# A graph layer with two ways to gather: compares one group ahead, picks ahead of the sums

## The chip, the core and the metric

The kernel runs on one core of a Trainium2 chip. The metric is the device time of one execution in microseconds (us), lower is better. TensorE multiplies matrices into PSUM, VectorE and ScalarE work element by element, GpSimd issues indirect DMAs here, and SyncE issues the other loads and the stores.

## What is computed

One layer of a graph network on 6250 nodes with 64 features and 206250 edges that are sorted by their destination:

```python
h = jnp.maximum(_layernorm(x, axis=-1), 0.0)
msg = jax.nn.relu(h[src] + edge_attr)
agg = jax.ops.segment_sum(msg, dst, num_segments=x.shape[0])
out = x + (jax.nn.relu((h + agg) @ W1 + b1) @ W2 + b2)
```

All of it is float32. The costly part is `h[src]`: a row of 64 numbers for each of 206250 edges.

## The kernel before, in words

The edges come in groups of 1024: 128 partitions by G = 8 columns, so a column is 128 edges. There are NG = 201 groups and a tail of 4 columns. For each group the edge features `ea` (SyncE) and the gathered source rows `xg` are brought to SBUF, into pools of LOOK = 10 buffers each.

A column's rows are fetched in one of two ways. `gather` (line 146) has GpSimd issue one indirect DMA per column from `h_rows`, the normalized nodes in DRAM. From group RAW = 4 on, the last columns of a group are left to TensorE: two in an even group, one in an odd one (`pool_cols`), 296 columns in all. They are called tiles here. For a tile, TensorE first turns the source numbers so that they lie along the free dimension (`spread`, line 304: a transpose into `turned`, a PSUM tile of 8 columns that is used as a ring). Then VectorE compares them with the numbers of all nodes (line 311), in four pieces (CUTS), and writes a 0/1 matrix `hot` of 49 blocks of 128 nodes. Then TensorE multiplies the 49 blocks with `hp`, the normalized nodes as three bf16 parts that add up to float32 (line 315, the picks). ScalarE puts the edge features of the tile beside the three parts as a fourth (line 360), and VectorE adds up the four (line 369).

For the other columns VectorE adds `xg` to the edge features in PSUM (line 367). ScalarE's relu makes the messages `msg` (line 371). They are summed by destination on TensorE: `one_hot` (line 341) compares the slot of each edge within a window of W = 64 nodes with the numbers 1 to 64, and 8 float32 matmuls (line 377) add the messages of a group into a PSUM window `agg`. VectorE adds the window to `z` at a place that is read from the data (line 336). The places of eight groups at a time are loaded into VectorE's registers (line 287). When all edges of a block of 512 nodes have been summed, `hidden`, `result` and `store` compute its output: two small products on TensorE, an add on VectorE (line 402), and a store; there are 12 such blocks and a rest of 106 nodes.

Each engine runs its instructions in the order of the program, and the program's order is the one that the Python code writes them in. Before the change, one step of the loop over groups is: add the last group's window to `z` and finish node blocks; `window_sum` (add, reduce, relu, sums of this group); `take` (load and copy the next group's edge features); `pick_group` (for each tile of the next group: turn the tile that comes four later, compare, pick); `one_hot` of the next group. The numbers 1 to 64 for the one-hot lie in PSUM (`wslots`).

Eight groups into the loop, `find_left` (lines 262 to 280) looks for edges outside their windows, which are done by another path if there are any; a step later the output bias is added to `x_sb` (line 433).

Of the kernel before, what the change touches and what calls it, by code (L numbers as in the profile page):

```python
# [9 lines left out]
F32 = mybir.dt.float32  # L10
I32 = mybir.dt.int32
I16 = mybir.dt.int16
BF16 = mybir.dt.bfloat16
# [6 lines left out]
P = 128  # L20
# [18 lines left out]
LAG = 1  # L39
AB = 4  # L40
KB = NB * R + 1
BIAS = 4096
# [8 lines left out]
def kernel(  # L51
# [62 lines left out]
    nc.vector.memset(ones, 1.0)  # L114
    wslots = psum.tile([P, W], F32, name="wslots", bufs=1)
    nc.vector.tensor_copy(wslots, slots[:, :W])

# [180 lines left out]
    nc.vector.tensor_scalar_add(src16, src_sb[:, :C], float(BIAS))  # L298
    turned = psum.tile([P, 8, P], BF16, name="turned", bufs=1)

    def spread(t):

        if t < len(tiles):
            nc.tensor.transpose(turned[:, t % 8, :],  # L304
                                src16[:, tiles[t]:tiles[t] + 1].bitcast(BF16).to_broadcast([P, P]), ident_b)

    def pick(t):
        oh = hot.tile([P, KB, P], BF16, name="hot")
        at = turned[:, t % 8, :].bitcast(I16)
        for k, to in zip(CUTS, CUTS[1:]):  # L310
            nc.vector.tensor_tensor(oh[:, k:to], at.unsqueeze(1).to_broadcast([P, to - k, P]),  # L311
                                    ids[:, k:to], ALU.is_equal)
        pk = psum.tile([P, 4, D], F32, name="pick", bufs=2)
        for k in range(KB):
            nc.tensor.matmul(pk[:, :3], oh[:, k, :], hp[:, k], start=(k == 0), stop=(k == KB - 1))  # L315
        return pk

# [13 lines left out]

    aggs, hots, taken, picks, banks = {}, {}, {}, {}, []

# [4 lines left out]
    def one_hot(g):  # L338
        n = G if g < NG else CT
        oh = work.tile([P, G, W], F32, name="oh")  # L340
        nc.vector.tensor_tensor(  # L341
            oh[:, :n], slot[:, cols_of(g)].unsqueeze(2).to_broadcast([P, n, W]),
            wslots.unsqueeze(1).to_broadcast([P, n, W]), ALU.is_equal)
        hots[g] = oh

    def take(g):

        n = pool_cols(g)
        ea, xg = loaded[g] if g < RAW else load(g)
        full = psum.tile([P, G, D], F32, name="full", bufs=2)  # L350
        nc.scalar.copy(full[:, :n], ea[:, :n])  # L351
        taken[g] = full, xg, ea

    def pick_group(g):

        for j in range(pool_cols(g), G if g < NG else 0):
            t = tile_no[g * G + j]
            spread(t + 4)
            picks[g, j] = pick(t)
            nc.scalar.copy(picks[g, j][:, 3], taken[g][2][:, j])  # L360

    def window_sum(g):
        n, m = (G, pool_cols(g)) if g < NG else (CT, CT)
        full, xg, _ = taken.pop(g)
        if g < RAW:
            norm_edges(xg)
        nc.vector.tensor_tensor(full[:, :m], full[:, :m], xg[:, :m], ALU.add)  # L367
        for j in range(m, n):
            nc.vector.tensor_reduce(full[:, j], picks.pop((g, j)).rearrange("p t d -> p d t"), AX.X, ALU.add)  # L369
        msg = work.tile([P, G, D], F32, name="msg")  # L370
        nc.scalar.activation(msg[:, :n], full[:, :n], AF.Relu)  # L371
        oh = hots.pop(g)
        if g % AB == 0:
# [41 lines left out]

    for t in range(4):
        spread(t)
    take(0)
    one_hot(0)
    for g in range(NG + 1):  # L420
        if g >= LAG:
            sum_into_z(g - LAG)
            blocks_behind(g - LAG)
        window_sum(g)
        if g + 1 <= NG:
            take(g + 1)
            pick_group(g + 1)
            one_hot(g + 1)
# [87 lines left out]
```

## Time and profile before

| | before |
|---|---|
| median of three runs | 2404.07 us (2403.34 to 2404.91) |
| the profiled execution, its own time | 2402.0 us |
| its span, first to last instruction | 2400.2 us |
| TensorE matmul busy | 1676.9 us, 70% |
| VectorE busy | 1510.9 us, 63% |
| GpSimd busy | 1251.4 us, 52% |
| ScalarE busy | 309.8 us, 13% |
| TensorE's granted clock, mean | 0.939 of 2.4 GHz |

The profile names engines PE (TensorE's matmuls), PEld (its weight loads), DVE (VectorE), ACT (ScalarE), POOL (GpSimd) and SP (SyncE); a q behind a name means the engine's sequencer. L315 is line 315. `xg<-h_rows,src_sb` reads: writes xg, reads h_rows and src_sb. In a timeline, instructions of one line that follow each other are merged (x49), and the time in front is the start.

### The profile page before, as it was taken

The page shows a single profiled execution, that of the slowest core. Times are in us where ns is not written, and L with a number is a line of the kernel's source. Part 1 is how long each engine was busy: PE and PEld are TensorE (multiplying, and loading weights), DVE is VectorE, ACT ScalarE, POOL GpSimd, SP SyncE. Part 2 cuts the span into 40 slices and gives each one's busy share as a digit, 9 for nine tenths or more (in the row PEclk, how much of TensorE's full clock was granted, in tenths as well). Part 3 has the DMA queues.
Part 4 walks back from the last instruction along what each step waited for, and adds up shares of the span by engine and source line. Part 5 has one row for each costly group of instructions (what it writes and reads, how often), then busy time and mean ns, then how long its engine had stood idle before and what let it go on. Part 6 is the DMA issues. An engine that isn't in the chain of part 4 may idle for free.

```text
span 2400.2 us, 43505 instructions
## 1 busy us (share of the span) xinstructions
PE 1676.9 (70%) x18201; PEld 1540.2 (64%) x18201; DVE 1510.9 (63%) x2208; ACT 309.8 (13%) x763; POOL 1251.4 (52%) x1325
## 2 busy tenths in 40 slices
PE   2456777777777777776777777777777777777777
PEld 1356666666666666666666666666666666666666
DVE  4566656656666666666666665666665666666666
ACT  4201111111111111111111111111111111111111
POOL 7775555555545545555555554554555555555510
PEclk9988999989999999999999999999998999999999
DMA  4211021121121121112112112102102112110200
GB/s 148 47 46 23 19 78 33 19 78 37 21 68 42 20 64 48 23 19 88 24 21 81 33 21 77 35 19 73 43 19 69 41 20 66 45 26 19 83 13 5
DMA packets 78190, 105.39 MB, mean 44 GB/s; under 512 B 26212, under 2 KB 30948, under 8 KB 77988
## 3 DMA queue, kind: packets, MB, share of 16 engines
q0 software_dynamic: 42112, 43.21, 9.1%
q1 hardware_dynamic: 34628, 57.65, 7.5%
q8 instruction: 144, 2.36, 0.4%
q10 hardware_dynamic: 1248, 1.70, 0.2%
q14 instruction: 58, 0.48, 0.1%
HBM read 99.26 MB, written 3.20 MB: 43 GB/s over the span
## 4 chain that ended last, share of the span: by engine, by line
PE 68%; DVE 18%; ACT 7%; issue 3%; POOL 1%; DVEq 1%; DMA 1%; ACTq 0%; SPq 0%
PE pick L315 55%; DVE hot L311 13%; PE agg L377 10%; ACT msg L371 5%; DVE full L369 4%; PE turned L304 2%; ACT pick L360 2%; POOL xg L146 1%; DVE full L367 1%; PE big L395 1%; PE big L385 1%; DVEq L287 1%; PE big L212 0%; ACT z L213 0%; DMA x_sb<-in_x_dram 0%
## 5 line engine op out<-in xcount | busy, mean ns | idle before, releaser
L146 POOL DMA_INDIRECT xg<-h_rows,src_sb x1284 | 1217.7, 948 | 1029.7 <-DVE full L367 678.3
L315 PE MATMUL pick<-hp,hot 128*128 128x192 bf16 x14504 | 1355.1, 258 | 327.1 <-DVE hot L311 327.1
L315 PEld LDWEIGHTS <-hot 128*128 128x128 bf16 x14504 | 1276.4, 103 | 385.8 <-DVE hot L311 373.0
L311 DVE TENSOR_TENSOR hot<-turned,ids 128x1536 bf16<-128x1536 int16 (+1 forms) x1184 | 1070.8, 967 | 677.1 <-PE turned L304 675.0
L377 PE MATMUL agg<-oh,msg 128*64 128x64 f32 x3224 | 243.7, 232 | 334.2 <-ACT msg L371 334.2
L377 PEld LDWEIGHTS agg<-oh,msg 128*64 128x64 f32 x3224 | 215.0, 144 | 386.7 <-ACT msg L371 386.7
L360 ACT COPY pick<-ea 128x64 f32<-128x64 f32 x296 | 63.9, 216 | 1865.9 <-PE pick L315 1865.9
L369 DVE TENSOR_REDUCE full<-pick 128x64 f32<-128x256 f32 x296 | 128.1, 433 | 118.3 <-ACT pick L360 105.4
L371 ACT ACTIVATE msg<-full 128x512 f32<-128x512 f32 x202 | 120.1, 595 | 142.6 <-DVE full L369 132.7
L341 DVE TENSOR_TENSOR oh<-slot,wslots 128x512 f32<-128x512 f32 x202 | 136.6, 676 | 0.0
L367 DVE TENSOR_TENSOR full<-full,xg 128x384 f32<-128x384 f32 (+1 forms) x202 | 118.8, 588 | 5.7 <-issue 4.8
L351 ACT COPY full<-ea 128x384 f32<-128x384 f32 (+1 forms) x202 | 103.5, 512 | 15.1 <-DMA ea<-in_edge_attr_dram 15.1
L304 PE MATMUL turned<-ident_b,src 128*128 128x128 bf16 x296 | 67.4, 230 | 3.1 <-DVE src L298 3.1
L336 DVE TENSOR_TENSOR z<-z,agg 64x64 f32 x202 | 41.9, 207 | 18.1 <-issue 8.7
L304 PEld LDWEIGHTS <-src 128*128 128x128 bf16 x296 | 28.6, 97 | 17.5 <-DVE src L298 3.6
L146 POOL DMA_INDIRECT xg<-in_x_dram,src_sb x32 | 32.3, 1008 | 12.3 <-issue 9.5
L212 PE MATMUL big<-ident,ln_h 128*64 128x128 f32 x48 | 12.7, 421 | 33.5 <-DVE ln_h L186 19.0
L212 PEld LDWEIGHTS big<-ident,ln_h 128*64 128x64 f32 x48 | 6.4, 159 | 39.4 <-issue 19.0
L402 DVE TENSOR_TENSOR o<-big,x_sb 128x256 f32<-128x256 f32 (+1 forms) x13 | 5.3, 409 | 24.8 <-PE big L395 24.8
L395 PE MATMUL big<-w_sb,h 64*128 64x64 f32 (+1 forms) x98 | 13.8, 281 | 0.4 <-ACT h L387 0.4
L213 ACT COPY z<-big 64x512 f32<-64x512 f32 x12 | 12.6, 1050 | 11.5 <-PE big L212 11.5
L385 PE MATMUL big<-z,w_sb 64*64 64x512 f32 (+1 forms) x26 | 13.4, 599 | 0.3 <-DVE z L336 0.3
(64 smaller groups left out, 106.2 us busy)
## 6 DMA issues: line engine op xcount, KB each, us to landing
ea<-in_edge_attr_dram SPq DMA_DIRECT2D x201, 256.0 KB, 3.1
xg<-h_rows,src_sb POOLq DMA_INDIRECT x1284, 2.5
x_sb<-in_x_dram SPq DMA_DIRECT2D x4, 384.0 KB
h_rows<-ln_h SPq DMA_DIRECT2D x4, 384.0 KB
out_dram<-o SPq DMA_DIRECT2D x12, 128.0 KB, 1.7
dst_sb<-in_dst_main_dram ACTq DMA_DIRECT2D x1, 804.0 KB
src_sb<-in_src_main_dram ACTq DMA_DIRECT2D x1, 788.0 KB
xg<-in_x_dram,src_sb POOLq DMA_INDIRECT x32, 3.1
```

The lines of the kernel that those rows point to most:

```text
L146: nc.gpsimd.indirect_dma_start(out=xg[:, j, :], out_offset=None, in_=rows[:, :], in_offset=bass.IndirectOffsetOnAxis(ap=idx[:, j:j + 1], a ...
L304: nc.tensor.transpose(turned[:, t % 8, :], src16[:, tiles[t]:tiles[t] + 1].bitcast(BF16).to_broadcast([P, P]), ident_b)
L311: nc.vector.tensor_tensor(oh[:, k:to], at.unsqueeze(1).to_broadcast([P, to - k, P]), ids[:, k:to], ALU.is_equal)
L315: nc.tensor.matmul(pk[:, :3], oh[:, k, :], hp[:, k], start=(k == 0), stop=(k == KB - 1))
L336: nc.vector.tensor_tensor(z[:, ds(at, W)], z[:, ds(at, W)], aggs.pop(g), ALU.add)
L341: nc.vector.tensor_tensor(oh[:, :n], slot[:, cols_of(g)].unsqueeze(2).to_broadcast([P, n, W]), wslots.unsqueeze(1).to_broadcast([P, n, W]) ...
L351: nc.scalar.copy(full[:, :n], ea[:, :n])
L360: nc.scalar.copy(picks[g, j][:, 3], taken[g][2][:, j])
L367: nc.vector.tensor_tensor(full[:, :m], full[:, :m], xg[:, :m], ALU.add)
L369: nc.vector.tensor_reduce(full[:, j], picks.pop((g, j)).rearrange("p t d -> p d t"), AX.X, ALU.add)
L371: nc.scalar.activation(msg[:, :n], full[:, :n], AF.Relu)
L377: nc.tensor.matmul(pa, msg[:, j, :], oh[:, j, :], start=(j == 0), stop=(j == n - 1))
```

## The change

The step of the loop is written anew. It now takes the next group, makes this group's messages (`messages`: add, reduce, relu), issues the picks of the next group (`pick`), adds the last group's window to `z` and finishes node blocks, issues this group's sums (`window_sum`), makes the compares of the group after next (`mark`), and the next group's one-hot. The transposes are done for 8 tiles at once into a PSUM tile of one bank, and there are two of these (`turned`, bufs=2). A group's one or two picked columns share one PSUM tile, with one copy of their edge features and one reduce. The bank for the second `turned` is that of `wslots`: the one-hot now reads the numbers 1 to 64 from `slots` in SBUF.

On VectorE, in the steady part, from the compare of an odd group's tile to the reduce, before (hot is the compare's result, oh the one-hot, z the sums of nodes, full the edge features in PSUM):

```order
L311 TENSOR_TENSOR hot<-turned,ids 128x1664 [waits PE_49]
L311 TENSOR_TENSOR hot<-turned,ids 128x1536 x3
L341 TENSOR_TENSOR oh<-slot,wslots 128x512
L336 ISA
L336 TENSOR_TENSOR z<-z,agg 64x64
L367 TENSOR_TENSOR full<-full,xg 128x448 [waits DMASW3_49,DMASW4_49,DMASW2_49,DMASW6_49,DMASW1_49,DMASW7_49,DMASW0_49,Activation_49]
L369 TENSOR_REDUCE full<-pick 128x64 [waits DVE_49,Activation_49]
```

and after the change:

```order
L376 TENSOR_TENSOR full<-full,xg 128x448 [waits DMASW3_49,DMASW5_49,DMASW2_49,DMASW6_49,DMASW1_49,DMASW7_49,DMASW0_49,Activation_49]
L378 TENSOR_REDUCE full<-pick 128x64 [waits DVE_49,PE_49,Activation_49]
L349 ISA
L349 TENSOR_TENSOR z<-z,agg 64x64 [waits PE_49]
L318 TENSOR_TENSOR hot<-turned,ids 128x1664
L318 TENSOR_TENSOR hot<-turned,ids 128x1536 x3
L354 TENSOR_TENSOR oh<-slot,slots 128x512
```

The compare stood ahead of the one-hot, the add into z and the add of gathered rows, and it waited for PE. Now it stands behind the reduce and the add into z, it waits for nothing of its own, and it is that of the group after next; the add into z has got a wait for PE, and so has the reduce.

On TensorE, around the sums of a group, before:

```order
L315 MATMUL pick<-hp,hot 128x192
L377 MATMUL agg<-oh,msg 64x64 [waits Activation_49]
L377 MATMUL agg<-oh,msg 64x64 x7
L304 LDWEIGHTS src_358
L304 MATMUL turned<-ident_b,src_358 128x128
L315 LDWEIGHTS hot [waits DVE_49]
L315 MATMUL pick<-hp,hot 128x192 [waits PE_49]
```

and after the change:

```order
L390 MATMUL agg<-oh,msg 64x64 [waits DVE_49,Activation_49]
L390 MATMUL agg<-oh,msg 64x64 x7
L329 LDWEIGHTS hot [waits DVE_49]
L329 MATMUL pick<-hp,hot 128x192 [waits Activation_49]
L329 LDWEIGHTS hot
L329 MATMUL pick<-hp,hot 128x192
```

Behind the sums stood one transpose and then the picks of the next group. Now the picks of the next group have been issued ahead of the sums, those of the group after next follow, and the transposes come eight at a time, in about one group of five.

```diff
--- before.py
+++ after.py
@@ -38,6 +38,7 @@
 LOOK = 10
 LAG = 1
 AB = 4
+TB = 8
 KB = NB * R + 1
 BIAS = 4096
 CUTS = (0, 13, 25, 37, KB)
@@ -112,8 +113,6 @@
                    allow_small_or_imprecise_dtypes=True)
     ones = const.tile([P, P], F32, name="ones")
     nc.vector.memset(ones, 1.0)
-    wslots = psum.tile([P, W], F32, name="wslots", bufs=1)
-    nc.vector.tensor_copy(wslots, slots[:, :W])
 
     ident_b = const.tile([P, P], BF16, name="ident_b")
     nc.vector.tensor_copy(ident_b, ident)
@@ -296,24 +295,38 @@
     ahead = {}
     src16 = const.tile([P, C], I16, name="src16")
     nc.vector.tensor_scalar_add(src16, src_sb[:, :C], float(BIAS))
-    turned = psum.tile([P, 8, P], BF16, name="turned", bufs=1)
-
-    def spread(t):
-
-        if t < len(tiles):
-            nc.tensor.transpose(turned[:, t % 8, :],
-                                src16[:, tiles[t]:tiles[t] + 1].bitcast(BF16).to_broadcast([P, P]), ident_b)
-
-    def pick(t):
-        oh = hot.tile([P, KB, P], BF16, name="hot")
-        at = turned[:, t % 8, :].bitcast(I16)
-        for k, to in zip(CUTS, CUTS[1:]):
-            nc.vector.tensor_tensor(oh[:, k:to], at.unsqueeze(1).to_broadcast([P, to - k, P]),
-                                    ids[:, k:to], ALU.is_equal)
-        pk = psum.tile([P, 4, D], F32, name="pick", bufs=2)
-        for k in range(KB):
-            nc.tensor.matmul(pk[:, :3], oh[:, k, :], hp[:, k], start=(k == 0), stop=(k == KB - 1))
-        return pk
+    turned, marks = {}, {}
+
+    def spread(b):
+
+        if b * TB < len(tiles):
+            turned[b] = psum.tile([P, TB, P], BF16, name="turned", bufs=2)
+            for k, c in enumerate(tiles[b * TB:(b + 1) * TB]):
+                nc.tensor.transpose(turned[b][:, k, :], src16[:, c:c + 1].bitcast(BF16).to_broadcast([P, P]), ident_b)
+
+    def tiles_of(g):
+        return [tile_no[g * G + j] for j in range(pool_cols(g), G)] if g < NG else []
+
+    def mark(g):
+        for t in tiles_of(g):
+            b, k = divmod(t, TB)
+            if k == 0:
+                spread(b + 1)
+            oh = hot.tile([P, KB, P], BF16, name="hot")
+            at = turned[b][:, k, :].bitcast(I16)
+            for k, to in zip(CUTS, CUTS[1:]):
+                nc.vector.tensor_tensor(oh[:, k:to], at.unsqueeze(1).to_broadcast([P, to - k, P]),
+                                        ids[:, k:to], ALU.is_equal)
+            marks[t] = oh
+
+    def pick(g):
+
+        ts = tiles_of(g)
+        pk = taken[g][2]
+        for i, t in enumerate(ts):
+            oh = marks.pop(t)
+            for k in range(KB):
+                nc.tensor.matmul(pk[:, i, :3], oh[:, k, :], hp[:, k], start=(k == 0), stop=(k == KB - 1))
 
     def norm_edges(xg):
         s = hot.tile([P, G], F32, name="raw_s")
@@ -329,7 +342,7 @@
         nc.vector.scalar_tensor_tensor(xg, xg, 0.0, v.unsqueeze(2).to_broadcast([P, G, D]),
                                        op0=ALU.max, op1=ALU.mult)
 
-    aggs, hots, taken, picks, banks = {}, {}, {}, {}, []
+    aggs, hots, taken, msgs, banks = {}, {}, {}, {}, []
 
     def sum_into_z(g):
         at = window_start(g)
@@ -340,7 +353,7 @@
         oh = work.tile([P, G, W], F32, name="oh")
         nc.vector.tensor_tensor(
             oh[:, :n], slot[:, cols_of(g)].unsqueeze(2).to_broadcast([P, n, W]),
-            wslots.unsqueeze(1).to_broadcast([P, n, W]), ALU.is_equal)
+            slots[:, :W].unsqueeze(1).to_broadcast([P, n, W]), ALU.is_equal)
         hots[g] = oh
 
     def take(g):
@@ -349,27 +362,27 @@
         ea, xg = loaded[g] if g < RAW else load(g)
         full = psum.tile([P, G, D], F32, name="full", bufs=2)
         nc.scalar.copy(full[:, :n], ea[:, :n])
-        taken[g] = full, xg, ea
-
-    def pick_group(g):
-
-        for j in range(pool_cols(g), G if g < NG else 0):
-            t = tile_no[g * G + j]
-            spread(t + 4)
-            picks[g, j] = pick(t)
-            nc.scalar.copy(picks[g, j][:, 3], taken[g][2][:, j])
-
-    def window_sum(g):
+        pk = None
+        if g < NG and n < G:
+            pk = psum.tile([P, 2, 4, D], F32, name="pick", bufs=2)
+            nc.scalar.copy(pk[:, :G - n, 3], ea[:, n:])
+        taken[g] = full, xg, pk
+
+    def messages(g):
         n, m = (G, pool_cols(g)) if g < NG else (CT, CT)
-        full, xg, _ = taken.pop(g)
+        full, xg, pk = taken.pop(g)
         if g < RAW:
             norm_edges(xg)
         nc.vector.tensor_tensor(full[:, :m], full[:, :m], xg[:, :m], ALU.add)
-        for j in range(m, n):
-            nc.vector.tensor_reduce(full[:, j], picks.pop((g, j)).rearrange("p t d -> p d t"), AX.X, ALU.add)
+        if m < n:
+            nc.vector.tensor_reduce(full[:, m:n], pk[:, :n - m].rearrange("p j t d -> p j d t"),
+                                    AX.X, ALU.add)
         msg = work.tile([P, G, D], F32, name="msg")
         nc.scalar.activation(msg[:, :n], full[:, :n], AF.Relu)
-        oh = hots.pop(g)
+        msgs[g] = msg
+
+    def window_sum(g):
+        n, oh, msg = G if g < NG else CT, hots.pop(g), msgs.pop(g)
         if g % AB == 0:
             banks.append(psum.tile([D, AB, W], F32, name="agg", bufs=1))
         pa = banks[-1][:, g % AB]
@@ -413,18 +426,23 @@
             if READY[c] == g:
                 hid[c] = hidden(c)
 
-    for t in range(4):
-        spread(t)
+    spread(0)
     take(0)
     one_hot(0)
+    mark(1)
     for g in range(NG + 1):
+        if g + 1 <= NG:
+            take(g + 1)
+        messages(g)
+        if g + 1 <= NG:
+            pick(g + 1)
         if g >= LAG:
             sum_into_z(g - LAG)
             blocks_behind(g - LAG)
         window_sum(g)
+        if g + 2 <= NG:
+            mark(g + 2)
         if g + 1 <= NG:
-            take(g + 1)
-            pick_group(g + 1)
             one_hot(g + 1)
         if g == 8:
             find_left()
```

## Rows read from the trace of the kernel before

**Rows 1.** The page: busy time of each engine; the chain by line.
```profile
PE 1676.9 (70%) x18201; PEld 1540.2 (64%) x18201; DVE 1510.9 (63%) x2208; ACT 309.8 (13%) x763; POOL 1251.4 (52%) x1325
...
PE pick L315 55%; DVE hot L311 13%; PE agg L377 10%; ACT msg L371 5%; DVE full L369 4%; PE turned L304 2%; ACT pick L360 2%; POOL xg L146 1%; DVE full L367 1%; PE big L395 1%; PE big L385 1%; DVEq L287 1%; PE big L212 0%; ACT z L213 0%; DMA x_sb<-in_x_dram 0%
```

**Rows 2.** Timeline 1199 to 1231 us: start, us, engine, line, what [idle before].
```profile
1199.42 3.62 DVE L311 TENSOR_TENSOR hot<-turned,ids 128x1664 bf16<-128x1664 int16 x4 [2.03 <-PE turned L304]
...
1208.61 5.79 PE L315 MATMUL pick<-hp,hot 128*128 128x192 bf16 x49 [1.12 <-DVE hot L311]
...
1215.57 4.22 PE L315 MATMUL pick<-hp,hot 128*128 128x192 bf16 x49 [1.12 <-DVE hot L311]
...
1221.25 1.15 PE L377 MATMUL agg<-oh,msg 128*64 128x64 f32 x16 [1.46 <-ACT msg L371]
...
1222.59 3.62 DVE L311 TENSOR_TENSOR hot<-turned,ids 128x1664 bf16<-128x1664 int16 x4 [2.03 <-PE turned L304]
```

**Rows 3.** Waits, whole run: us in total, times, longest.
```profile
POOL xg L146 <- DVE full L367: 678.3, 178, 11.4
DVE hot L311 <- PE turned L304: 675.0, 291, 4.6
...
POOL xg L146 <- issue: 341.6, 1120, 0.6
PE agg L377 <- ACT msg L371: 334.2, 202, 7.5
PE pick L315 <- DVE hot L311: 327.1, 292, 1.1
```

**Rows 4.** Timeline 2360 to 2400 us, the end of the run.
```profile
2361.17 8.26 PE L315 MATMUL pick<-hp,hot 128*128 128x192 bf16 x98 [1.12 <-DVE hot L311]
...
2370.11 3.61 DVE L311 TENSOR_TENSOR hot<-turned,ids 128x1664 bf16<-128x1664 int16 x4
...
2378.71 8.26 PE L315 MATMUL pick<-hp,hot 128*128 128x192 bf16 x98
...
2391.78 0.42 DVE L367 TENSOR_TENSOR full<-full,xg 128x256 f32<-128x256 f32 x1
```

**Rows 5.** The page's groups: busy us, mean ns, then idle before.
```profile
L146 POOL DMA_INDIRECT xg<-h_rows,src_sb x1284 | 1217.7, 948 | 1029.7 <-DVE full L367 678.3
...
L369 DVE TENSOR_REDUCE full<-pick 128x64 f32<-128x256 f32 x296 | 128.1, 433 | 118.3 <-ACT pick L360 105.4
...
L341 DVE TENSOR_TENSOR oh<-slot,wslots 128x512 f32<-128x512 f32 x202 | 136.6, 676 | 0.0
L367 DVE TENSOR_TENSOR full<-full,xg 128x384 f32<-128x384 f32 (+1 forms) x202 | 118.8, 588 | 5.7 <-issue 4.8
...
L336 DVE TENSOR_TENSOR z<-z,agg 64x64 f32 x202 | 41.9, 207 | 18.1 <-issue 8.7
```

**Rows 6.** Timeline 160 to 205 us, around the check for left-over edges.
```profile
167.01 1.84 DVE L263 SCALAR_TENSOR_TENSOR left<-slot,left 128x1612 f32<-128x1612 f32 x1
...
168.09 1.58 POOL L146 DMA_INDIRECT xg<-h_rows,src_sb  x1 [0.30 <-issue]
168.88 1.84 DVE L264 SCALAR_TENSOR_TENSOR left<-dst_sb,left 128x1612 f32<-128x1612 int32 x1
169.97 1.57 POOL L146 DMA_INDIRECT xg<-h_rows,src_sb  x1 [0.30 <-issue]
...
178.20 0.21 DVE L336 TENSOR_TENSOR z<-z,agg 64x64 f32 x1 [4.17 <-issue]
```

**Rows 7.** Groups, shapes apart: 512 elements with two operands in SBUF.
```profile
L322 DVE TENSOR_TENSOR xg<-xg,raw_s 128x512 f32<-128x512 f32 x4 | 2.8, 692 | 0.1
```

**Rows 8.** Timeline 0 to 130 us: the first gather from normalized rows.
```profile
46.96 0.95 POOL L146 DMA_INDIRECT xg<-h_rows,src_sb  x1 [0.31 <-issue]
```

**Rows 9.** The page's DMA issues: count, us from issue to landing.
```profile
xg<-h_rows,src_sb POOLq DMA_INDIRECT x1284, 2.5
```

**Rows 10.** Busy time 1208.6 to 1214.4 us; 0.72 is the granted clock.
```profile
1208.60:1214.40 5.80, 5.79 (x50) 5.49 (x50) 2.54 (x3) 0.00 (x0) 3.77 (x4) 0.72 0.14 28
```

## The prediction

> **What bounds the kernel now.** I read the page's chain first [rows 1]. No engine is full (TensorE is busy for 70%, VectorE for 63%), and more than half of the chain is picks on TensorE (55%); then come VectorE's compares (13%), the sums on TensorE (10%), the relu (5%) and the reduce (4%). These are the steps of one group, one behind the other: the chain changes engine all the time. So the question is not which engine is slow but which steps could lie beside each other.
>
> The timeline of one pair of groups shows that [rows 2]. A pair has three picked columns (two in the even group, one in the odd), and the reader is to see one period from the compare at 1199.42 us to the one at 1222.59 us: 23.17 us. There are 98.5 such pairs, 2282 us, so 118 us of the 2400.2 lie outside of them. Its compares stand behind idle stretches of VectorE, 2.03 us at both ends of this period, that end with a transpose of line 304; the run has 291 of them [rows 3]. That transpose is not even for this compare: it fills the column that the compare four tiles later reads, but it lies in the same tile `turned`, and on TensorE it stands behind the picks of the tile before. So a compare waits for those picks to end, and its own picks wait 1.12 us for the first of its four pieces. Only the other three pieces lie beside picks. Behind a group's last pick come reduce and relu, and TensorE waits 1.46 us before the sums.
>
> The waits in total [rows 3] give the size of it: VectorE 675.0 us for transposes; TensorE 327.1 us for first pieces and 334.2 us for messages. GpSimd waits 678.3 us for the add that frees a buffer of gathered rows. Its pace now is that of the others, ten groups ahead of them, and not its own.
>
> The end of the run tells what the first wait is worth [rows 4]. There are no tiles left to turn there, so the compare at 2370.11 has no idle time in front of it, and from the picks at 2361.17 to those at 2378.71 a pair takes 17.54 us, with the waits for messages still in it.
>
> **The change part by part.** Compares are made for the group after next, from a turned tile of their own bank, and the picks of the next group stand ahead of this group's sums. All three waits of TensorE and VectorE then have other work in them. What is left is each engine's own work for a pair:
>
> - *TensorE*: two tiles of picks 8.26 us [rows 4], one tile 4.22 us [rows 2], two groups of sums at 1.15 us [rows 2], and the transposes, 2% of the span by the chain, 0.5 us: **15.3 us**. Their number does not change; eight now come together.
> - *VectorE*: three compares at 3.62 us [rows 2], two one-hots at 0.676, two adds into z at 0.207, two adds of gathered rows at 0.588 and one reduce at 0.433 us [rows 5] make 14.24 us. The reduce of two columns at once is in no row: 0.433 us if width costs nothing, 0.866 us if it costs all; I take the middle, 0.65. **14.9 us**. Two things lose their cover. The load of eight window starts stood behind the compares and ahead of the add into z, so the compares hid it; now it stands behind the reduce, with the compares behind it. The one place where nothing hid it had 4.17 us [rows 6]; 26 loads are at most 108 us or 1.1 us a pair, and nothing where VectorE has time to spare. And the output add of a node block, which waits for its products, now finds the next group's picks ahead of those on TensorE: at most 8.26 us, 12 times, 1.0 us a pair. So VectorE lies between 14.7 us (the narrow bound of the reduce, all else covered) and 17.0 (nothing covered), and the compares queued behind these waits are what TensorE would miss.
> - *GpSimd*: 13 gathers at 0.948 us [rows 5] with 341.6 us over 1120 gaps, 0.305 us each, between them [rows 3]: **16.3 us**. Nothing in the order of its gathers changes.
> - *ScalarE* copies the edge features of a group's picked columns at once: fewer instructions on an engine that is 13% busy [rows 1]. I cost it at nothing; the picks of a whole group cover it. SyncE's loads keep their ten buffers.
>
> So GpSimd is late next. Its waits for buffers go as soon as the others need less than its own time for a pair, and it began ahead of them.
>
> One edit touches GpSimd itself. The one-hot's second operand moves from PSUM to SBUF, so that both operands lie there. For VectorE an instruction of this size with two SBUF operands takes 0.692 us [rows 7], against 0.676 now: nothing. But look at the stretch where VectorE works on two SBUF operands [rows 6]: the gathers at 168.09 and 169.97 took 1.58 and 1.57 us, and each ended 0.82 us after the end of the VectorE instruction in which it began (167.01 + 1.84 = 168.85 to 169.67; 168.88 + 1.84 = 170.72 to 171.54). The mean over all is 0.948 [rows 5]. So a gather that reaches a point some 0.13 us after its start while such an instruction runs stands still until that ends. The one-hots of before, with an operand in PSUM, left that mean alone. With a new one-hot of 0.69 us and a gather each 1.253 us, 55% of them catch one, for 0.345 us on the average: 0.19 us each, **38 us** for 202. The bounds are nothing (the two never meet, since VectorE keeps step with the landings) and 0.69 us each, 139 us.
>
> A rule of the Trainium skill speaks the other way. Its page "SBUF — State Buffer", section "Who interferes with whom", says that a VectorE instruction with two SBUF inputs contends with GpSimd instructions that read SBUF and not with those that only write, and infers that writing DMA descriptors is not held up by a `tensor_tensor`. By that rule the 38 us would be nothing. Rows 6 don't agree: there two-input instructions stretched both gathers by over 0.6 us.
>
> **The sum.** The first gather from the normalized rows starts at 46.96 us [rows 8]. 1284 of them at 1.253 us put the start of the last at 46.96 + 1283 × 1.253 = 1654.5 us. It lands 2.5 us after issue [rows 9], at 1657.0, and from the last add of gathered rows to the end of the span were 8.4 us (2391.78 to 2400.2) [rows 4]: 1665.4. With the 38 us of stretched gathers the span is 1703.8. The profiled execution took 1.8 us more than its span, and the median of the runs shown is 2.1 us above it: **1708 us**.
>
> **The rivals.**
>
> *GpSimd is not held up by the one-hots.* VectorE's step is set by the landing of gathers, so its one-hots come at a fixed phase to them, and this phase may be one where they never meet; nothing in the trace tells it. Without the 38 us: 1670 us, and TensorE's chain would stand there too, 118 + 98.5 × 15.3 = 1625, so it can't go far below. Chance 0.15. The rule of the Trainium skill above gives the same time.
>
> *VectorE sets the pace.* If the loads of window starts and the output adds cost their full price, a pair takes 17.0 us, more than GpSimd's 16.3 + 0.4: 118 + 98.5 × 17.0 = 1793, 1797 with what lies around it. For it: both stand ahead of the compares. Against: they come once in 8 and 16 groups, and up to ten groups of gathers wait in buffers meanwhile. Chance 0.20, from 1740 on.
>
> *The compare doesn't come off the path.* The change would not do what it says if TensorE still found its compares late, for instance because three hot buffers tie a compare to the picks three tiles before. Then the pair is at best the 17.54 us of the end: 118 + 98.5 × 17.54 = 1846, 1850 in all. The order speaks against it: the reduce that stands ahead of those compares has waited for those picks already. Chance 0.05.
>
> *Slower: the lower clock.* At one tile of this very pair the picks took 5.79 us instead of 4.22, in a stretch with a granted clock of 0.72 [rows 10]; ahead of it TensorE had stood still for the message and for the compare. Time goes with the inverse of the clock (5.79 × 0.72 = 4.17), so at 1.2 GHz TensorE's 15.3 us become 30.6. If the shorter, more frequent gaps of the new order left it at the lower level for 51% of its work (15.3 × 1.51 = 23.1), all gain would be gone; at 60% the run takes 118 + 98.5 × 24.5 = 2531 us. The mean now is 0.939 with 30% of idle time; I expect less idle time, hence 0.02.
>
> **How the numbers follow.** The forecast (GpSimd back to back, one-hots costing 10 to 70 us) has 0.58, the rivals 0.15, 0.20, 0.05 and 0.02. The likeliest gives 1708. The range takes in the case without stretched gathers, less a little for gaps that I took too wide, and VectorE's full price: 1650 to 1800; outside are the last two rivals and the tails of the others. Faster by over 0.2% (about what a measurement of this kernel tells from no change) are all cases but the last and a share of mishaps not named: 0.96, within 0.01, slower 0.03.
>
> **What would show it.** Right: GpSimd's wait for the add of gathered rows near zero after the first pairs, gathers 1.25 us apart, and VectorE's add waiting for landings instead; the wait of the compare for transposes gone; gathers of up to 1.6 us all along the run, each over a one-hot. The picks' wait for compares and the sums' wait for messages small. Wrong: GpSimd still waiting hundreds of us for adds (VectorE or TensorE sets the pace), gathers of 0.95 us throughout, or a granted clock well under 0.9.

## The result, and the profile after

| | before | after |
|---|---|---|
| median of four runs each | 2404.11 us | 1732.43 us (1731.46 to 1734.59) |
| the profiled execution's span | 2400.2 us | 1730.3 us |
| TensorE's granted clock, mean | 0.939 | 0.965 |

The ratio is 0.7207, interval 0.7195 to 0.722: the change takes off 672 us, and 1732 lies within the range, 24 us above the number forecast.

The page after: busy time of each engine, then groups (busy us, mean ns of one, and idle time before them) that answer to [rows 1, 5]:

```profile
PE 1538.0 (89%) x18201; PEld 1466.3 (85%) x18201; DVE 1468.2 (85%) x2108; ACT 298.9 (17%) x664; POOL 1313.3 (76%) x1325
...
L145 POOL DMA_INDIRECT xg<-h_rows,src_sb x1284 | 1279.0, 996 | 391.3 <-issue 339.8
L329 PE MATMUL pick<-hp,hot 128*128 128x192 bf16 x14504 | 1264.3, 250 | 46.2 <-ACT pick L368 45.9
...
L378 DVE TENSOR_REDUCE full<-pick 128x128 f32<-128x512 f32 x197 | 111.6, 567 | 35.8 <-PE pick L329 11.6
L354 DVE TENSOR_TENSOR oh<-slot,slots 128x512 f32<-128x512 f32 x202 | 136.1, 674 | 0.0
```

TensorE and VectorE are now busy for 89% and 85%. GpSimd's gathers have 391.3 us of idle time before them instead of 1029.7, and take 996 ns instead of 948.

The waits after (us in total, times, longest), which answer to [rows 3]:

```profile
POOL xg L145 <- issue: 349.3, 1146, 0.3
ACT full L364 <- DMA ea<-in_edge_attr_dram: 79.7, 11, 8.5
DVE z L349 <- issue: 70.2, 18, 4.2
...
PE pick L329 <- ACT pick L368: 45.9, 19, 4.5
...
DVE o L415 <- PE big L408: 34.3, 12, 4.0
PE agg L390 <- ACT msg L381: 30.3, 24, 5.1
DVE full L376 <- DMA xg<-h_rows,src_sb: 30.2, 15, 6.1
...
DVE z L349 <- PE pick L329: 27.2, 7, 4.2
```

GpSimd's wait for adds, 678.3 us before, has left the list, as has the compares' wait for transposes, 675.0 us; the picks' wait for compares is down from 327.1 to 0.3 us, and the sums' wait for messages fell from 334.2 to 30.3 us. New are ScalarE's wait for edge features (15.1 us before, 79.7 now) and with it that of TensorE's picks (45.9). New as well are VectorE's 25 waits ahead of the add into z, where it loads window starts: the profile puts 18 of them down to "issue" (70.2 us) and 7 to a pick (27.2 us).

From the timeline of the whole run, GpSimd's first and last gather from the normalized rows, and VectorE's adds of gathered rows for groups 22, 136, 200 and the tail:

```profile
48.32 0.94 POOL L145 DMA_INDIRECT xg<-h_rows,src_sb  x1 [0.30 <-issue]
...
257.02 0.55 DVE L376 TENSOR_TENSOR full<-full,xg 128x384 f32<-128x384 f32 x1
...
1178.79 0.57 DVE L376 TENSOR_TENSOR full<-full,xg 128x384 f32<-128x384 f32 x1 [0.21 <-DMA xg<-h_rows,src_sb]
...
1714.91 0.57 DVE L376 TENSOR_TENSOR full<-full,xg 128x384 f32<-128x384 f32 x1 [6.11 <-DMA xg<-h_rows,src_sb]
...
1717.42 0.95 POOL L145 DMA_INDIRECT xg<-h_rows,src_sb  x1 [0.30 <-issue]
...
1720.32 0.43 DVE L376 TENSOR_TENSOR full<-full,xg 128x256 f32<-128x256 f32 x1 [3.56 <-DMA xg<-h_rows,src_sb]
```

From 48.32 to 1717.42 us GpSimd never paused for more than 0.4 us. Unstretched, 1283 steps of 0.944 + 0.304 us are 1601.2 us; it took 1669.1. The 68 us between are stretched gathers, 174 of them. So the forecast's skeleton stands: GpSimd issues back to back, and the one-hots hold it up. How much they hold it up is what the forecast had wrong.

In the timeline from 1014 to 1032 us, every one-hot (L354) has a held gather (L145) upon it:

```profile
1015.35 0.67 DVE L354 TENSOR_TENSOR oh<-slot,slots 128x512 f32<-128x512 f32 x1
1015.56 1.29 POOL L145 DMA_INDIRECT xg<-h_rows,src_sb  x1 [0.30 <-DMA xg<-h_rows,src_sb]
...
1016.63 0.70 DVE L378 TENSOR_REDUCE full<-pick 128x128 f32<-128x512 f32 x1
1017.15 0.94 POOL L145 DMA_INDIRECT xg<-h_rows,src_sb  x1 [0.30 <-issue]
...
1023.39 0.95 POOL L145 DMA_INDIRECT xg<-h_rows,src_sb  x1 [0.30 <-issue]
1024.42 0.67 DVE L354 TENSOR_TENSOR oh<-slot,slots 128x512 f32<-128x512 f32 x1
1024.64 1.27 POOL L145 DMA_INDIRECT xg<-h_rows,src_sb  x1 [0.30 <-issue]
...
1029.77 0.67 DVE L354 TENSOR_TENSOR oh<-slot,slots 128x512 f32<-128x512 f32 x1
1029.96 1.30 POOL L145 DMA_INDIRECT xg<-h_rows,src_sb  x1 [0.31 <-issue]
...
1031.05 0.70 DVE L378 TENSOR_REDUCE full<-pick 128x128 f32<-128x512 f32 x1
```

The one-hot of 1015.35 ends at 1016.02, and the gather that began within it ends 0.83 us after that, at 1016.85, after 1.29 us instead of 0.94. The next starts at 1017.15. From there on six gathers come each 1.247 us after the other, undisturbed, and the seventh starts at 1024.64: again within a one-hot, which came 9.07 us after the first. A held gather with its gap and six free ones make 1.59 + 6 × 1.247 = 9.07 us. The one-hot after that comes 5.35 us later, and a held gather, its gap and three free ones make 1.58 + 3 × 1.247 = 5.32. The holding itself sets the phase of the gathers anew, and VectorE's intervals happen to be such that the next one-hot is met too. The whole run bears this out: behind a one-hot that had caught a gather the next one caught one in 133 of 159 cases (84%), and behind one that hadn't, in 25 of 42 (60%, near the 55% of a chance meeting).

Of the 202 one-hots 159 caught a gather, for 0.385 us on the average: 61 us. Two of these gathers, 1.24 and 4.46 us of the 61, were held on by the instructions of the left-over check and of the output bias that follow their one-hots; those hold a gather with the one-hot on ScalarE too. The other 157 come to 55.5 us, 0.354 us each.

### The profile page after: what moved, and what is told of

Same layout as the page of the kernel before. It is cut to its first block, busy times and chain, and to the rows that moved or that the text cites. A ratio compares the mean times of both kernels' runs of the same rounds, so it can differ in the third digit from the quotient of the medians.

```text
span 1730.3 us, 43209 instructions
## 1 busy us (share of the span) xinstructions
PE 1538.0 (89%) x18201; PEld 1466.3 (85%) x18201; DVE 1468.2 (85%) x2108; ACT 298.9 (17%) x664; POOL 1313.3 (76%) x1325
## 5 line engine op out<-in xcount | busy, mean ns | idle before, releaser
L145 POOL DMA_INDIRECT xg<-h_rows,src_sb x1284 | 1279.0, 996 | 391.3 <-issue 339.8
L329 PE MATMUL pick<-hp,hot 128*128 128x192 bf16 x14504 | 1264.3, 250 | 46.2 <-ACT pick L368 45.9
L329 PEld LDWEIGHTS <-hot 128*128 128x128 bf16 x14504 | 1218.7, 99 | 62.0 <-issue 42.4
L318 DVE TENSOR_TENSOR hot<-turned,ids 128x1536 bf16<-128x1536 int16 (+1 forms) x1184 | 1058.9, 957 | 0.0
L390 PE MATMUL agg<-oh,msg 128*64 128x64 f32 x3224 | 235.4, 228 | 50.5 <-ACT msg L381 30.3
L378 DVE TENSOR_REDUCE full<-pick 128x128 f32<-128x512 f32 x197 | 111.6, 567 | 35.8 <-PE pick L329 11.6
L354 DVE TENSOR_TENSOR oh<-slot,slots 128x512 f32<-128x512 f32 x202 | 136.1, 674 | 0.0
L349 DVE TENSOR_TENSOR z<-z,agg 64x64 f32 x202 | 41.5, 205 | 102.7 <-issue 70.2
L364 ACT COPY full<-ea 128x384 f32<-128x384 f32 (+1 forms) x202 | 102.9, 510 | 85.3 <-DMA ea<-in_edge_attr_dram 79.7
L368 ACT COPY pick<-ea 128x128 f32<-128x128 f32 x197 | 46.4, 236 | 0.0
L305 PE MATMUL turned<-ident_b,src 128*128 128x128 bf16 x296 | 24.8, 232 | 21.1 <-DVE hot L318 18.0
L145 POOL DMA_INDIRECT xg<-in_x_dram,src_sb x32 | 32.8, 1024 | 13.1 <-issue 9.5
L305 PEld LDWEIGHTS <-src 128*128 128x128 bf16 x296 | 19.0, 103 | 23.9 <-issue 17.8
L415 DVE TENSOR_TENSOR o<-big,x_sb 128x256 f32<-128x256 f32 (+1 forms) x13 | 5.3, 408 | 34.3 <-PE big L408 34.3
L408 PE MATMUL big<-w_sb,h 64*128 64x64 f32 (+1 forms) x98 | 14.7, 293 | 0.4 <-ACT h L400 0.4
L408 PEld LDWEIGHTS big<-w_sb,h 64*128 64x128 f32 (+1 forms) x98 | 12.8, 200 | 2.6 <-issue 1.7
```

Of the source, the lines that this page charges most:

```text
L145: nc.gpsimd.indirect_dma_start(out=xg[:, j, :], out_offset=None, in_=rows[:, :], in_offset=bass.IndirectOffsetOnAxis(ap=idx[:, j:j + 1], a ...
L305: nc.tensor.transpose(turned[b][:, k, :], src16[:, c:c + 1].bitcast(BF16).to_broadcast([P, P]), ident_b)
L329: nc.tensor.matmul(pk[:, i, :3], oh[:, k, :], hp[:, k], start=(k == 0), stop=(k == KB - 1))
L349: nc.vector.tensor_tensor(z[:, ds(at, W)], z[:, ds(at, W)], aggs.pop(g), ALU.add)
L354: nc.vector.tensor_tensor(oh[:, :n], slot[:, cols_of(g)].unsqueeze(2).to_broadcast([P, n, W]), slots[:, :W].unsqueeze(1).to_broadcast([P, ...
L368: nc.scalar.copy(pk[:, :G - n, 3], ea[:, n:])
```

## The experiments

**One-hot on ScalarE.** The numbers are whole, so relu(1 − (number − slot)²) is 1 where they agree and 0 elsewhere. ScalarE makes it with eight squares and a relu, a step earlier in the program. That leaves VectorE no instruction with two SBUF operands in the steady part.

```diff
-        nc.vector.tensor_tensor(
-            oh[:, :n], slot[:, cols_of(g)].unsqueeze(2).to_broadcast([P, n, W]),
-            slots[:, :W].unsqueeze(1).to_broadcast([P, n, W]), ALU.is_equal)
+        for j in range(n):
+            nc.scalar.activation(oh[:, j], slots[:, :W], AF.Square, bias=slot[:, g * G + j:g * G + j + 1], scale=-1.0)
+        nc.scalar.activation(oh[:, :n], oh[:, :n], AF.Relu, bias=ones[:, 0:1], scale=-1.0)
...
             take(g + 1)
+            one_hot(g + 1)
```

> The one-hot on ScalarE once more, since the kernel before itself took 3254 us beside the first run of it. GpSimd sets the pace: no gather is stretched any more, the mean gather is at 950 ns instead of 996, and the time falls by the 61 us of stretches, 1671 (1660 to 1690). ScalarE's work is longer than I took it there, 337 ns for a column of the one-hot and 723 for its relu, 3.4 us a group and 5.0 with relu and copies: it fits in the shortest step of a group, 5.3 us, but barely, and if it delays the messages or the copies that picks wait for, the time lies between 1690 and 1760. VectorE sets the pace (rival): 121 us of its work are gone, 1611 to 1640 unless GpSimd's 1660 stops it.

Measured: 1671.7 us (1671.48 to 1672.45), ratio to before 0.6955, interval 0.6943 to 0.6966. The page:

```profile
PE 1525.9 (91%) x18201; PEld 1457.6 (87%) x18201; DVE 1348.3 (81%) x1906; ACT 836.2 (50%) x2478; POOL 1253.9 (75%) x1325
...
L145 POOL DMA_INDIRECT xg<-h_rows,src_sb x1284 | 1220.0, 950 | 391.3 <-issue 338.9
...
L355 ACT ACTIVATE oh<-slots,slot 128x64 f32<-128x64 f32 x1612 | 406.2, 334 | 0.0
...
L356 ACT ACTIVATE oh<-oh,ones 128x512 f32<-128x512 f32 x202 | 145.6, 721 | 6.6
```

Gathers take 950 ns again, none is held by a one-hot, and the last one starts at 1657.05 us; the forecast's own term for that, without stretched gathers, was 1654.5. It beats both kernels. But the edit also takes 120 us of work off VectorE (1348.3 instead of 1468.2), so it doesn't yet tell which of the two made the 61 us.

**The one-hot's operand back in PSUM.** VectorE keeps its work; the second operand is a piece of the turned sources, which lie in PSUM.

```diff
-            slots[:, :W].unsqueeze(1).to_broadcast([P, n, W]), ALU.is_equal)
+            turned[max(turned)][:, 0, :].bitcast(F32).unsqueeze(1).to_broadcast([P, n, W]), ALU.is_equal)
```

> The one-hot's second operand from PSUM (the true one-hot is left out), for the fourth time: the kernel before itself took over 3200 us beside the first three. With the one-hot on ScalarE the time was 1671.7 us, but that edit also takes 121 us of work from VectorE. GpSimd alone sets the pace: 1671 here too. VectorE and TensorE at 16.17 us a pair close behind it: 1718 (1708 to 1725), and of the 61 us of ScalarE's version some 45 are VectorE's relief and not the gathers'.

Measured: 1706.94 us (1706.62 to 1707.25), ratio 0.7107, interval 0.7087 to 0.7128. The page, and the end of the run in the timeline:

```profile
PE 1528.8 (90%) x18201; PEld 1459.7 (86%) x18201; DVE 1465.2 (86%) x2108; ACT 298.8 (18%) x664; POOL 1254.3 (74%) x1325
...
L145 POOL DMA_INDIRECT xg<-h_rows,src_sb x1284 | 1220.6, 951 | 391.3 <-issue 331.3
...
L354 DVE TENSOR_TENSOR oh<-slot,turned 128x512 f32<-128x512 f32 x202 | 134.3, 665 | 23.3 <-PE turned L305 23.3
```

```profile
1657.44 0.94 POOL L145 DMA_INDIRECT xg<-h_rows,src_sb  x1 [0.30 <-issue]
1661.24 0.66 DVE L354 TENSOR_TENSOR oh<-slot,turned 128x512 f32<-128x512 f32 x1
1661.83 0.62 DVE L376 TENSOR_TENSOR full<-full,xg 128x448 f32<-128x448 f32 x1
...
1694.82 0.43 DVE L376 TENSOR_TENSOR full<-full,xg 128x256 f32<-128x256 f32 x1
```

The operand's place is shown as the cause of the stretching: with 202 one-hots of the same shape and nearly the same length (665 ns against 674), gathers take 951 ns. 101 gathers began within a one-hot there, and only the one over the left-over check was stretched. But the span falls only from 1730.3 to 1704.8. GpSimd issues its last gather at 1657.44, and the add for it comes at 1694.82, 37 us behind; all along the run the adds stand 37 to 65 us behind their last gathers, so they wait for no landing. From the add of group 22 to that of group 190 a pair takes 16.21 us, and it is VectorE and TensorE that need this time. So GpSimd alone is refuted, and 1707 lies a microsecond below the range of the other theory. But 9 waits of the one-hot for the borrowed operand, 23.3 us, belong to the experiment: without them the time might be as low as 1684 (an estimate, if nothing covers them). So of the 61 us that the kernel with ScalarE gains, 25 to 49 come from freeing the gathers alone; the other 12 to 35 needed VectorE's relief as well. In the kernel with ScalarE the pair takes 15.74 us up to group 136, the adds catch up with the gathers at group 184, and from then on stand 2.5 to 5 us behind.

Read in this light, the end of the changed kernel is GpSimd's, which never pauses. Its adds are 40 to 55 us behind the gathers up to group 22, come at 16.17 us a pair from there (257.02 us) to group 136 (1178.79), and have caught up then; from there on they are 2.5 to 8 us behind, at GpSimd's 16.8 us a pair. VectorE and TensorE set the pace of the adds in the first two thirds, but not the time of the run. They are close enough behind GpSimd that taking the stretches away shows only in part.

**Two turned banks alone.** The kernel before, with the two PSUM tiles of eight turned columns and the one-hot's SBUF operand, in the old order:

```diff
-    turned = psum.tile([P, 8, P], BF16, name="turned", bufs=1)
...
+            turned[b] = psum.tile([P, TB, P], BF16, name="turned", bufs=2)
...
-            spread(t + 4)
+            if t % TB == 0:
+                spread(t // TB + 1)
```

> The kernel before with the two turned banks alone (eight transposes at once, one-hot from SBUF); compares, picks and sums in the old order. Beside its first run the kernel before took 3315 us, so it is run once more. The pair of the end of the run, 17.54 us, should hold all along: 118 + 98.5 x 17.54 = 1846 (1820 to 1880), so the banks bring most and the order the last 100 us. If the order of picks and compares is what counts, it stays above 2200.

Measured: 1922.25 us (1921.50 to 1923.01), ratio 0.8001, interval 0.7977 to 0.8024. The waits:

```profile
PE agg L378 <- ACT msg L372: 329.8, 202, 7.5
DVE full L370 <- ACT pick L361: 317.3, 186, 4.2
POOL xg L145 <- DVE full L368: 184.9, 101, 6.6
```

The compares' wait for transposes is gone as expected, and that alone is 480 of the 672 us; the wait of the sums for messages is as long as before. The time expected was 76 us too low: I took the 17.54 us a pair of the run's end [rows 4], where there is no node block and no load left; from group 22 to 136 a pair took 18.22. The new order and the merged copies and reduces are worth the other 190 us. The one-hot has both operands in SBUF here too, and yet it costs the gathers only 14 us: 88 one-hots held one, for 0.16 us on the average. GpSimd waits for an add 101 times in this run and then starts behind it; that this gives the two a phase at which they do each other little harm is a reading that no run tested.

**Runs that decide nothing.** Nine runs were made beside runs of the kernel before that took 3220 to 3337 us instead of 2404, so they can't be set beside those above. Which chip it was doesn't explain it: chip 7 is on record both for the first four of them, beside 3254 us, and for the two banks alone at 1922 us, beside 2402. The same two experiments came first there. The one with ScalarE took 2921.29 us:

> The one-hot moves to ScalarE: a square of slot minus number for each of 8 columns, then relu(1 - square), exact for whole numbers, issued behind the copies of the next group. GpSimd sets the pace: as without the stretch, 1671 (1660 to 1690), and VectorE is busy 121 us less. If ScalarE's 2.4 us more a group delay relu or the copies that the picks wait for, up to 1750. VectorE sets the pace: 121 us of VectorE's work are gone, 1611 to 1640 unless GpSimd's 1660 stops it.

The one with the operand in PSUM was run three times; it took 2834.06, 2894.21 and 2841.84 us:

> The changed kernel with one edit: the one-hot's second operand is read from a turned tile in PSUM instead of slots in SBUF. The length of the instruction stays, but the sums are of other edges (the one-hot itself is left out). GpSimd sets the pace (theory): 159 of the gathers lose a stretch of 0.385 us each, the mean gather falls from 996 to about 950 ns, and the time falls by the same 61 us, to 1671 (1660 to 1685). VectorE or TensorE sets the pace (rival): gathers lose the stretch too, but GpSimd then waits for buffers, and the time stays above 1715.

> The changed kernel with one edit: the one-hot's second operand is read from a turned tile in PSUM instead of slots in SBUF. The length of the instruction stays, but the sums are of other edges (the true one-hot is left out). GpSimd alone sets the pace: the 61 us of stretched gathers go from the time, 1671. A second theory has come up from the changed kernel's trace: from the add of group 22 (257.0 us) to that of group 136 (1178.8) VectorE and TensorE took 16.17 us a pair while gathers were ready, close behind GpSimd's 16.9. By it the time falls to 257.0 + 89.5 x 16.17 and some 14 us of tail, 1718 (1708 to 1725), with GpSimd waiting for buffers or far ahead at the end.

> The one-hot's second operand from PSUM once more (the true one-hot is left out), since the kernel before itself took over 3200 us beside its two runs so far. GpSimd alone sets the pace: 1671. VectorE and TensorE at 16.17 us a pair close behind it: 1718 (1708 to 1725).

The two banks alone took 2765.97 us:

> The kernel before with the two turned banks alone (eight transposes at once, one-hot from SBUF); compares, picks and sums in the old order. The pair of the end of the run, 17.54 us, should hold all along: 118 + 98.5 x 17.54 = 1846 (1820 to 1880). If the order of picks and compares is what counts, it stays above 2200.

A second one-hot ahead of the first, to double VectorE's load, took 2816.55 us:

```diff
+        nc.vector.tensor_tensor(
+            oh[:, :n], slot[:, cols_of(g)].unsqueeze(2).to_broadcast([P, n, W]),
+            turned[max(turned)][:, 0, :].bitcast(F32).unsqueeze(1).to_broadcast([P, n, W]), ALU.is_equal)
```

> A second one-hot ahead of each one-hot, into the same kind of tile, with its second operand in PSUM: 0.6 us more for VectorE in each of 202 groups, 121 us, and nothing for GpSimd. GpSimd sets the pace: VectorE's spare time takes most of it, 1732 to 1750. VectorE sets the pace: 1732 + 121 = 1853.

One gather fewer in each group, to shorten GpSimd's path, took 2520.12 and 2556.35 us:

```diff
-        gather(xg, src_sb[:, cols_of(g)], pool_cols(g), x if g < RAW else h_rows)
+        gather(xg, src_sb[:, cols_of(g)], pool_cols(g) - (RAW <= g < NG), x if g < RAW else h_rows)
```

> One gather fewer in each of 197 groups; that column keeps its edge features alone, so its source rows are left out. GpSimd's path is 197 x 1.25 = 246 us shorter. GpSimd sets the pace: the time falls until the next limit, the chain of VectorE and TensorE, which I put at 15.3 to 16.0 us a pair with some 110 us outside, 1615 to 1690, and GpSimd waits for buffers again. VectorE or TensorE sets the pace: above 1715.

> One gather fewer in each of 197 groups; that column keeps its edge features alone, so its source rows are left out. GpSimd's path is 246 us shorter. GpSimd alone with much room behind it: 1615 to 1690. The second theory (VectorE and TensorE at 16.17 us a pair close behind): 1718 (1700 to 1725), and GpSimd waits for buffers again.

And the compares directly ahead of their picks, not a group ahead, took 2881.05 us:

```diff
         if g + 1 <= NG:
+            mark(g + 1)
             pick(g + 1)
...
-        if g + 2 <= NG:
-            mark(g + 2)
```

> The changed kernel with the compare of the next group right ahead of its picks instead of a group earlier. TensorE then waits in each group for the reduce and the first piece of the compare behind the last picks (0.43 or 0.70 us and 1.04 us), of which 1.15 us are filled by the sums: 16.0 to 16.5 us a pair. GpSimd sets the pace: within 20 us of 1732. If the head start of a group is what matters: 1850 to 2000.

All nine took far longer than any time that was expected; the bounds left open upward ("above 1715", "above 2200") they meet without deciding anything. The trace says why the theories were not at stake: TensorE was late by itself. From the third run of the kernel with the operand in PSUM, the timeline of TensorE and GpSimd:

```profile
707.67 0.32 PE L329 MATMUL pick<-hp,hot 128*128 128x192 bf16 x1 [0.94 <-issue]
...
708.39 0.33 PE L329 MATMUL pick<-hp,hot 128*128 128x192 bf16 x1 [0.40 <-issue]
...
711.33 0.95 POOL L145 DMA_INDIRECT xg<-h_rows,src_sb  x1 [0.30 <-issue]
...
714.70 4.00 PE L329 MATMUL pick<-hp,hot 128*128 128x192 bf16 x24 [0.91 <-issue]
...
720.66 8.25 PE L329 MATMUL pick<-hp,hot 128*128 128x192 bf16 x98
...
723.44 0.95 POOL L145 DMA_INDIRECT xg<-h_rows,src_sb  x1 [11.17 <-DVE full L376]
```

From 703 to 714 us the picks come one, two or three at a time, 0.7 to 1.4 us apart; at 720.66 there are 98 of them in 8.25 us, as in the other traces. The profile gives "issue" as what ended the gaps, no engine and no DMA. The slow stretch runs while GpSimd issues gathers, the quick one while GpSimd waits 11.17 us for an add, and the next slow one begins behind the gathers of 723.44. GpSimd waits 1017 to 1199 us for adds in these runs. Gathers took 948 to 952 ns in all of them, wherever the one-hot's operand lay: they come in bursts, and only 5 to 58 of the 202 one-hots with two SBUF operands had a gather begin within them, against 168 in the changed kernel. What the doubled one-hot, a gather fewer or a late compare would do where the kernel before takes 2404 us is open; they were not tried there.

## Why the prediction was right, and where it was not

- **The path (right).** That the three waits go, that GpSimd's own pace is late next and that it never waits for an add in the steady part: all as said. The first gather was taken at 46.96 us and came at 48.32; the tail from the last gather to the end of the span was taken at 10.9 us and was 12.9.
- **The one-hot term (mis-sized).** "55% of them catch one, for 0.345 us on the average": 38 us. Measured: 159 of 202, 79%, for 0.385 us: 61 us; without the two that other instructions held on, 0.354 us, so the length was right and the share was not. The step that failed is that the two meet at random. The gather that was held starts its successors from the end of the one-hot, and so the next meeting isn't random: 84% behind a caught gather, 60% behind none. Of the 26.5 us by which the span came out longer, 23.5 are in the stretch of gathers, 1.4 at the start and 2.0 in the tail (together 0.4 more than 26.5, by rounding).
- **The rule weighed against it (decided).** By what the Trainium skill, "SBUF — State Buffer", section "Who interferes with whom", infers for descriptor writing beside a `tensor_tensor`, these 61 us would be nothing. The trace differs: two-input one-hots stretched 159 gathers, and with the operand in PSUM none was stretched by a one-hot. The gathers read their row numbers from `src_sb` in SBUF; by which of their accesses they are held, no run shows. The forecast took the side of [rows 6], rightly.
- **"TensorE's chain would stand there too, 118 + 98.5 × 15.3 = 1625" (wrong).** That counted TensorE's own work in a pair and nothing that comes between. Without stretched gathers, and with the one-hot still on VectorE, the kernel stands at 1707 (1684 by the estimate above), not at 1670. An undisturbed pair does take less than I summed, 14.42 us between two-column reduces (1016.63 to 1031.05) against 14.9 and 15.3, as instructions on VectorE begin before the one ahead has ended (1661.24 + 0.66 against 1661.83 in the trace with the PSUM operand). But from group 22 to 136 it was 16.17.
- **"VectorE sets the pace" (right in kind; one of its two prices was right).** The loads of window starts did lose their cover, nearly at the full price: 25 of the 26 stand open at 3.84 to 4.21 us, the last at 0.95, 98.4 us in all (bound: 108). The output adds cost 34.3 us (bound: 1.0 us a pair, 98). The reduce of two columns took 0.70 us, where I chose 0.65. VectorE's waits from the add of group 22 to that of group 136 (257.02 to 1178.79 us), which are 57 pairs:

```profile
DVE z L349 <- issue: 35.3, 9, 4.2
DVE o L415 <- PE big L408: 25.6, 7, 4.0
DVE z L349 <- PE pick L329: 19.5, 5, 4.2
DVE full L378 <- PE pick L329: 9.5, 8, 1.7
```

The loads take 54.8 us of it, the output adds 25.6 and late picks 9.5: 1.58 us a pair, nearly all of the 1.75 between 14.42 and 16.17 us. 17.0 needed the output adds at full price too. It was a near thing: with the 38 us that the forecast gave to the one-hots GpSimd would have ended at 1703.8, and the kernel without stretched gathers, held by VectorE and TensorE, ends at 1704.8, some of it the experiment's own. How near this limit lay the forecast couldn't tell (14.7 to 17.0 us a pair), and in so far its hit is luck.
- **"SyncE's loads keep their ten buffers", costed at nothing (wrong).** Here the timeline around a node block shows a wait that the prediction doesn't have:

```profile
1043.61 1.10 PE L408 MATMUL big<-w_sb,h 64*128 64x64 f32 x8
...
1044.75 0.42 DVE L415 TENSOR_TENSOR o<-big,x_sb 128x256 f32<-128x256 f32 x1 [4.02 <-PE big L408]
...
1045.20 0.34 SPq L417 DMA_DIRECT2D out_dram<-o  x1
...
1045.64 6.63 SPq L136 DMA_DIRECT2D ea<-in_edge_attr_dram  x12
...
1049.76 0.54 ACT L364 COPY full<-ea 128x448 f32<-128x448 f32 x1 [8.51 <-DMA ea<-in_edge_attr_dram]
...
1050.49 5.70 PE L329 MATMUL pick<-hp,hot 128*128 128x192 bf16 x48 [4.15 <-ACT pick L368]
```

The products of a node block (L408) stand behind the next group's 98 picks; the output add waits 4.02 us for them, and the store for the add. On SyncE's queue the loads of edge features wait behind the store: SyncE had issued none since 956 us, while the buffers were used up, and 12 of them follow the store at once. ScalarE lacks them for 8.51 us and TensorE its copy for 4.15 us. That happens 11 times: 79.7 us on ScalarE, 43.8 on TensorE. Little of it gets further: VectorE waits for late picks for only 9.5 us between groups 22 and 136. So the wait was left out of the forecast, and no run shows that it costs the run any time.
- **The clock (right).** Less idle time of TensorE, and a mean of 0.965; the slower rival had nothing behind it.

## What to carry to other kernels

When a wait is taken away and another engine runs back to back, look at every instruction that can hold that engine up: a hold-up of 0.4 us that used to fall into idle time is now paid each time, and two regular streams that hold each other up don't meet at random. Price the limit behind the new one with everything that comes only once in 8 or 16 steps, since undisturbed steps make it look further off than it is (14.42 us against 16.2). An operand's place can be worth more than an instruction's length: with one operand in PSUM the one-hot was 9 ns shorter and the run 25 us, though with borrowed numbers in place of the right ones. Moving the one-hot from VectorE to a ScalarE that was busy for 17% keeps the right numbers and gave 61 us.

## What the runs showed of the hardware

The locked phase was not expected: 159 of 202 VectorE instructions of 0.67 us with two SBUF operands held a gather, for 0.385 us on the average, and the held gather's end moved the whole stream so that it met the next. Nor was it expected that in some runs TensorE issues its matmuls 0.7 to 1.4 us apart while GpSimd issues gathers, at a mean granted clock of 0.64 (703 to 714 us in the trace above), and back to back when it doesn't: 0.17 us each at first, with 0.56 granted from 714 to 720.6 us, then 0.084 us each at 1.00. The kernel before takes 3220 to 3337 us beside these runs instead of 2404; on chip 7 it took 3254 us at one time and 2402 at another. The overlap is what the traces show; its cause wasn't found.
